# Moved denominator sums, moved stores and a new closing step in a two-layer graph network

## The chip, the cores and the metric

The kernel runs on one core of a Trainium2 chip. The metric is the device time of one execution in microseconds; lower is better. Before the change three executions took 3256.42, 3258.72 and 3258.72 us; the median is 3258.72. One further execution was recorded by the hardware profiler: it took 3257.38 us, of which the profile's span covers 3255.6.

The engines are named as in the profile: PE multiplies matrices (PEld loads its weights), DVE and ACT work element by element on 128 partitions, POOL and SP are used here mainly to issue DMA transfers. A name with a q (ACTq, SPq, POOLq) is an engine's instruction queue, where it issues a transfer.

## The reference

Two graph layers act on 4096 nodes with 512 features (4 heads of 128). The mask `adj` is the same 4096 x 4096 matrix of zeros and ones in both. Cut to what matters:

```python
h = relu(layernorm(x))
# layer 0: two attentions with the same weights, an MLP after each
Xw  = einsum('hnd,hde->hne', heads(h), W)
sig = sigmoid(f1[:, :, None] + f2[:, None, :])     # f1, f2 = Xw . V
att = softmax of sig where adj != 0, else 0        # both masks are adj
Xn  = batchnorm(att @ Xw)                          # the encoder attention
emb = batchnorm(elu(Xn @ Wenc.T + b) + Xn)
Yc  = elu((att @ emb) @ W.T)                       # the decoder attention
x   = x + batchnorm(elu(Yc @ Wdec.T + b) + Yc)
# layer 1: graph attention
h = relu(layernorm(x))
feats  = einsum('nf,hfo->hno', h, W1)
logits = leaky_relu(e_s[:, :, None] + e_n[:, None, :], 0.2)
attn   = softmax of logits where adj != 0
out    = x + relu(attn @ feats + b)
```

## The kernel before

All node data stand transposed: features on partitions, nodes along the row. A softmax is never formed as such. The kernel makes unnormalised weights, multiplies the values with them on PE, sums the weights over the source nodes (the denominator), and multiplies the products by the reciprocal of that sum.

**Stages.** Features (layer norm, transposes and the products with W, lines 465 to 552); encoder attention; the encoder's MLP and the decoder's values; decoder attention; the decoder's MLP, the residual and the second layer's features; graph attention (GAT). The three attentions share the function `attention` (L221). In the features' stage the products of two heads stand side by side in one PSUM bank, 130 columns each (128 values and 2 scores); L541 copies the values of each head to `R[0]` to `R[3]`, on ACT but for the last copies, which DVE makes. The order of instructions on an engine is the order of the program, except where the scheduler that builds the kernel finds another; `issue_after` and `pinned` keep an instruction behind a named one.

**Blocks and tiles.** An attention has 8 blocks, one for each head and half of the target nodes (2048). A block has 32 tiles, one for each 128 source nodes. A tile of weights `e` is 128 x 2048 floats. It is made by ACT and masked by DVE: in the encoder and decoder a tanh (L450) and an exp (L451) on ACT and a product with the mask (L452) on DVE; in the GAT a relu (L905) on ACT and one DVE instruction (L906) that adds, and masks. The mask tile `a` (bytes) is loaded by SP (L210) into one of five buffers. PE then multiplies: four matmuls of 512 columns for each tile (L371; for the first two tiles of a block the fourth follows at L368, since its PSUM bank is still in use by the block before). In the last block of the encoder and of the GAT the last tiles (one and two) are held back as `late` and multiplied bank by bank at L423.

**The program's order.** Weights of a tile are made in the order of the loop, with 8 buffers for `e` in the encoder, 6 in the decoder, 9 in the GAT, two of them shared by all three, so that the next attention's first two tiles can be made while the one before ends. What is done with a block's results is put into a list, `later`, and called some tiles into the next block.

**Denominators.** For each block the encoder and the GAT say which tiles are summed how:

```python
moved, by_ones, *ends_later = modes(n) if modes is not None else ((), ())
```

A tile in `moved` is added into a second accumulator (`acc2` in the encoder, `w` or a part of `R[2]` in the GAT) by two accumulating DMAs that POOL issues (L386). A tile in `by_ones` is summed by PE: four matmuls with ones (L262). All others DVE adds into `acc` (L392, L394). At the block's end PE sums the accumulators in the same way. The tables are ENC_FIRST for the encoder's first block, ENC_SECOND for its second (n = 1), ENC for the six after these; GAT_FIRST, GAT (six middle blocks) and GAT_LAST for the GAT. The decoder has no sums: it reads the reciprocals of the encoder. The reciprocals of a block take a way through DRAM in the next block, a "hop": copied, written, read back in another shape, inverted, written, and spread over the partitions (L269, L274, L278, L282, L287), by POOL's queue in the encoder and decoder, by ACT's in the GAT.

**Kept tiles.** Every fifth masked tile of the encoder (j = 4, 9, ...) is stored to DRAM, `ekeep`, three tiles after it was made, by ACT's queue (L358, and L410 and L412 for the last of a block), and loaded by SP in the decoder (L343) in place of being made again.

**A last block** has no next one. In the encoder and the GAT the denominators are copied on DVE with a lower bound (in the GAT with a small number added) and inverted (L434, L435), then PE spreads each bank's reciprocals over the partitions by a matmul with `ident` (L440). In the GAT each bank then takes four operations: ACT copies it out of PSUM with `ssum` added (L911), DVE multiplies (L915), ACT adds the bias with a relu (L918), DVE adds the residual (L921); then it is stored.

## Time and profile before

| what | us |
| --- | --- |
| median of the three runs | 3258.72 |
| profiled execution | 3257.38 |
| its span in the profile | 3255.6 |
| features, start to 66 | 66 |
| encoder attention, 62 to 1047 | 985 |
| encoder's MLP and decoder's values, 1047 to 1217 | 170 |
| decoder attention, 1217 to 2077 | 860 |
| decoder's MLP, residual, second features, 2077 to 2330 | 253 |
| GAT, 2330 to 3256 | 926 |

The stages overlap by a few tiles, and their bounds are rounded. Busy time in two of the stretches (start:end, length, then the busy time of PE, PEld, DVE, ACT and POOL with the number of instructions, the granted clock of PE, the busy share of the 16 DMA engines and the GB/s that they moved):

```
1028.00:1047.00 19.00, 16.70 (x62) 6.09 (x60) 16.15 (x12) 9.72 (x11) 0.00 (x0) 1.00 0.37 121
2330.00:3256.00 926.00, 915.97 (x2305) 394.94 (x2303) 897.16 (x451) 572.67 (x337) 197.78 (x232) 1.00 0.90 214
```

Three further forms of line are used below. A group is a set of instructions of one kind on one line (line, engine, operation, the output and input tiles, size, then busy time, count, mean time of one). In a list of waits stand the waiting instruction, an arrow, the instruction that released it, and the sum in us, the number and the longest of such waits. In a timeline stand the start, the length, the engine with the line, the tiles, the count of like instructions in a row, and in brackets how long the engine stood before and for whom.

### The profile page before, as it was taken

The numbers are of one execution on the slowest core, as the hardware profiler recorded it, in microseconds if no ns is written. First come the engines' busy times: TensorE is split into PE (matmuls) and PEld (weight loads), VectorE is DVE, ScalarE is ACT, GpSimd is POOL, SyncE is SP. The second block draws the span as 40 slices with busy tenths as digits, with TensorE's granted clock in tenths as the row PEclk, the third lists the DMA queues.
The fourth block names the chain that finished last, engine by engine and source line by source line (L and its number), as shares of the span: only waits on it lengthen the run. The fifth ranks groups of instructions, "written<-read, shape, count | busy, mean of one in ns | idle before, by whom it ended". The sixth has DMA issues, their size and how long they took to land.

```text
span 3255.6 us, 26153 instructions
## 1 busy us (share of the span) xinstructions
PE 3197.0 (98%) x8755; PEld 1483.5 (46%) x8755; DVE 2661.1 (82%) x1953; ACT 2597.9 (80%) x1884; POOL 478.7 (15%) x622
## 2 busy tenths in 40 slices
PE   7999999999999999999999999999999999999999
PEld 6334434444444464444444444448644444444443
DVE  7999999999999665556655665585699999999998
ACT  7999999999997459899999999566765666666664
POOL 2001211211211000000000000025412222222221
PEclk9999999999999999999999999999999999999999
DMA  9998988988986023433443443231489999889985
GB/s 210 197 196 229 268 227 224 270 230 220 271 234 162 2 68 132 146 129 133 145 147 120 137 155 121 77 123 58 128 204 219 219 226 241 220 206 236 221 216 142
DMA packets 211153, 578.51 MB, mean 178 GB/s; under 512 B 25069, under 2 KB 28173, under 8 KB 195017
## 3 DMA queue, kind: packets, MB, share of 16 engines
q0 software_dynamic: 67968, 222.51, 36.0%
q1 hardware_dynamic: 126432, 293.72, 26.5%
q10 hardware_dynamic: 16616, 60.60, 4.8%
q8 instruction: 69, 1.13, 0.1%
q14 instruction: 68, 0.55, 0.0%
HBM read 377.10 MB, written 84.29 MB: 142 GB/s over the span
## 4 chain that ended last, share of the span: by engine, by line
PE 67%; DVE 15%; issue 7%; ACT 6%; DMA 5%; POOL 0%; DVEq 0%; ACTq 0%; POOLq 0%
PE ps L371 51%; DVE e L452 9%; PE ps L615 7%; PE ps L811 3%; ACT e L450 3%; DMA a<-mask 3%; DVE acc L394 2%; ACT e L451 2%; DMA acc<-e 1%; PE den L262 1%; DVE R L394 1%; PE ps L672 1%; DVE e L906 1%; PE ps L368 1%; PE ps L537 1%
## 5 line engine op out<-in xcount | busy, mean ns | idle before, releaser
L371 PE MATMUL ps<-e,R 128*128 128x512 f32 x6024 | 2612.8, 594 | 34.8 <-DVE e L452 32.6
L371 PEld LDWEIGHTS ps<-e,R 128*128 128x128 f32 x6024 | 1139.8, 190 | 1500.7 <-issue 1398.1
L452 DVE TENSOR_TENSOR e<-e,a 128x2048 f32<-128x2048 f32 (+1 forms) x470 | 1052.2, 2261 | 391.2 <-ACT e L451 373.5
L450 ACT ACTIVATE e<-rowb,score 128x2048 f32<-128x2048 f32 (+1 forms) x470 | 912.3, 1967 | 86.2 <-PE ps L371 45.6
L451 ACT ACTIVATE e<-e 128x2048 f32<-128x2048 f32 (+1 forms) x470 | 870.5, 1879 | 6.1
L905 ACT ACTIVATE e<-rowb,nq,jcol 128x2048 f32<-128x2048 f32 x224 | 461.9, 2090 | 273.5 <-DMA w<-e 124.9
L906 DVE SCALAR_TENSOR_TENSOR e<-e,jcol,a 128x2048 f32<-128x2048 f32 (+1 forms) x265 | 593.6, 2280 | 7.7 <-ACT e L905 7.7
L394 DVE TENSOR_TENSOR acc<-acc,e 128x2048 f32<-128x2048 f32 x126 | 288.1, 2286 | 2.0
L394 DVE TENSOR_TENSOR R<-R,e 128x2048 f32<-128x2048 f32 x123 | 282.1, 2294 | 0.0
L386 POOL DMA_DIRECT2D w<-e x178 | 150.7, 849 | 612.5 <-DMA w<-e 356.3
L615 PE MATMUL ps<-R,w 128*128 128x512 f32 x512 | 220.3, 592 | 0.7 <-DVE w L573 0.7
L386 POOL DMA_DIRECT2D acc<-e x144 | 120.7, 883 | 536.5 <-DMA acc<-e 193.0
L287 POOL DMA_DIRECT2D rb<-rinvs x60 | 34.6, 582 | 1060.8 <-DVE R L563 867.5
L615 PEld LDWEIGHTS ps<-R,w 128*128 128x128 f32 x512 | 97.2, 190 | 122.7 <-issue 117.9
L636 ACT ACTIVATE ex<-ps,bias 128x512 f32<-128x512 f32 x64 | 44.0, 688 | 98.5 <-PE ps L615 78.7
L811 PE MATMUL ps<-w1x,hT 128*128 128x260 f32 x512 | 115.5, 384 | 1.4 <-ACT hT L789 1.4
L811 PEld LDWEIGHTS ps<-w1x,hT 128*128 128x128 f32 x512 | 96.5, 190 | 19.9 <-issue 3.3
L905 ACT ACTIVATE e<-w,nq,jcol 128x2048 f32<-128x2048 f32 (+1 forms) x41 | 67.4, 1710 | 24.9 <-DMA R<-e 24.9
L638 DVE SCALAR_TENSOR_TENSOR ex<-ex,re 128x512 f32<-128x512 f32 x64 | 45.0, 703 | 36.4 <-ACT re L637 36.2
L848 POOL TENSOR_TENSOR vacc<-vacc,R 128x128 f32<-128x128 f32 x120 | 65.9, 579 | 45.2 <-ACT R L841 44.8
L841 ACT ACTIVATE R<-ps,rstd 128x128 f32<-128x128 f32 x128 | 38.7, 371 | 29.2 <-PE ps L811 25.4
L262 PE MATMUL den<-e,ones 128*32 128x512 f32 x456 | 54.9, 598 | 0.0
(173 smaller groups left out, 1246.5 us busy)
## 6 DMA issues: line engine op xcount, KB each, us to landing
a<-mask SPq DMA_DIRECT2D x720, 256.0 KB, 4.2
w<-e POOLq DMA_DIRECT2D x178, 512.0 KB, 6.7
acc<-e POOLq DMA_DIRECT2D x144, 512.0 KB, 6.7
ekeep<-e ACTq DMA_DIRECT2D x48, 1024.0 KB, 7.8
e<-ekeep SPq DMA_DIRECT2D x48, 1024.0 KB, 4.8
mask<-in_adjT POOLq DMA_DIRECT2D x8, 2048.0 KB, 102.3
rowb<-rows SPq DMA_DIRECT2D x16, 1024.0 KB, 7.0
rb<-rinvs POOLq DMA_DIRECT2D x60, 256.0 KB, 4.0
```

Source lines behind the costliest of these rows:

```text
L262: last_ones = nc.tensor.matmul(den[s * 32:(s + 1) * 32, :], ones[:, 0:32], t[:, s * IB:(s + 1) * IB], start=start, stop=stop)
L371: last_main = nc.tensor.matmul(b, block(values[h], j), e[:, s * IB:(s + 1) * IB], start=(j == 0), stop=(j == NJ - 1))
L386: nc.gpsimd.dma_start(into_half, e_half, **({"accum_op": ALU.add} if j > moved[0] else {}))
L394: nc.vector.tensor_add(acc, acc, e)
L450: nc.scalar.activation(e, rowb, AF.Tanh, bias=column(score[:, 1], j, h), scale=0.5)
L451: last_act = nc.scalar.activation(e, e, AF.Exp, scale=0.5)
L452: last_dve = nc.vector.tensor_mul(e, e, a)
L615: last = nc.tensor.matmul(z, w[:, fb, o * P:(o + 1) * P], nodes(src[fb], ib), start=(fb == 0), stop=(fb == C - 1))
L811: m = nc.tensor.matmul(banks[k][:, 0:2 * DX], hT[:, fb, c * P:(c + 1) * P], w1x[:, fb, 2 * k:2 * k + 2, :].rearrange("p h x -> p (h x)"), ...
L848: nc.gpsimd.tensor_add(vacc[:, h, :], vacc[:, h, :], block(v1[h], j))
L905: last_act = nc.scalar.activation(e, rowb, AF.Relu, bias=column(nq, j, h), scale=column(jcol, j, h))
L906: last_dve = nc.vector.scalar_tensor_tensor(e, e, column(jcol2, j, h), a, ALU.add, ALU.mult)
```

## The change

- The copies out of PSUM: `R[0]` to `R[4]` become parts of one tile `RS`, and one instruction copies the values of two heads (104 copies on ACT become 52, 24 on DVE become 12).
- The encoder attention may start behind the features' last copy on ACT, `last_copy`, in place of the last relu; in the built order the tanh table's load and a quarter of the first tile's tanh then stand ahead of the last four relus.
- ENC_SECOND: other tiles in both lists, and seven moved tiles in place of six.
- From the third block on the stores of kept tiles go from ACT's queue to SP's, five tiles after their tile was made in place of three (36 of 48 stores), as do those left at a block's end.
- In the encoder's last block the additions of tiles j >= 26 that DVE makes (26 to 29) are put off to the last tile; in the built order the masks of 27 to 29 stand ahead of them, one addition follows, then the masks of 30 and 31, then three additions.
- The decoder's first two masks are kept behind a `bn_stats` in the encoder's MLP (`behind`).
- GAT: the middle blocks sum tile 31 alone by PE, tile 30 by DVE. The last block sums 30 and 31 by PE in place of 12, and holds back four tiles in place of two.
- The GAT's last block ends in `finish_gat`: the reciprocals go to DRAM and are spread back by SP's queue into `R[2]`, each bank takes two DVE instructions that read PSUM directly, and the bias is added to the residual beforehand. The matmuls at L440 and the ACT operations fall away there.

```diff
@@ -60,13 +60,13 @@
-ENC_SECOND = (13, 15, 17, 20, 22, 25), (5, 6, 10, 11, 23, 24, 30, 31)
+ENC_SECOND = (12, 14, 17, 19, 22, 24, 26), (1, 2, 4, 5, 7, 8, 30, 31)
 ENC = (0, 2, 5, 7, 10, 12, 15, 17, 20, 22, 25), (8, 9, 30, 31)
 GAT_FIRST = (0, 2, 4, 6, 8, 10, 12, 14, 16, 18, 20, 22, 24), (30, 31)
-GAT = tuple(range(3, 28, 2)), (30, 31), True
-GAT_LAST = (3, 5, 7, 9, 11, 13, 15, 17, 19, 21, 23), (12,)
+GAT = tuple(range(3, 28, 2)), (31,), True
+GAT_LAST = (3, 5, 7, 9, 11, 13, 15, 17, 19, 21, 23), (30, 31)
@@ -92,7 +92,8 @@
-    R = [big.tile([P, N], FP, name=f"R{i}") for i in range(5)]
+    RS = big.tile([P, 5, N], FP, name="R")
+    R = [RS[:, i, :] for i in range(5)]
@@ -326,7 +330,7 @@
-            adds, held, stores, next_row = [], [], [], None
+            adds, held, stores, at_end, next_row = [], [], [], [], None
             for j in range(NJ):
@@ -348,14 +352,16 @@
-                    with pinned(products_of[:1] if kept == "read" and n == 0 and j < 8 else []):
+                    with pinned([*(products_of[:1] if kept == "read" and n == 0 and j < 8 else ()),
+                                 *(behind if n == 0 and j < EP else ())]):
                         products_of = weights(e, rowb, a, j, h, SB if NJ * n + j < in_parts0 else 1)
+                    if stores and (store if n > 1 else j % KEEP == KEEP - 3):
+                        k, t = stores.pop()
+                        (nc.sync if n > 1 else nc.scalar).dma_start(ekeep[h][tb][k], t)
                     if store:
                         stores.append((j // KEEP, e))
-                    if j % KEEP == KEEP - 3 and stores:
-                        k, t = stores.pop()
-                        nc.scalar.dma_start(ekeep[h][tb][k], t)
                 def products():
@@ -373,7 +379,7 @@
-                if last and invert is not None and j >= NJ - (1 if kept is not None else 2):
+                if last and invert is not None and j >= NJ - (1 if kept is not None else 4):
@@ -388,10 +394,16 @@
-                        if len(adds) == 2:
+                        if last and kept is not None and j >= NJ - 6:
+                            at_end.append(e)
+                        elif len(adds) == 2:
                             nc.vector.tensor_add(acc, *adds)
...
                             nc.vector.tensor_add(acc, acc, e)
+                    if j == NJ - 1:
+                        for t in at_end:
+                            nc.vector.tensor_add(acc, acc, t)
                     if held and j + 1 not in by_ones:
@@ -407,9 +419,9 @@
                 if last:
-                    nc.scalar.dma_start(ekeep[h][tb][k], t)
+                    nc.sync.dma_start(ekeep[h][tb][k], t)
                 else:
-                    at(EVICT, nc.scalar.dma_start, ekeep[h][tb][k], t)
+                    at(EVICT, (nc.sync if n > 1 else nc.scalar).dma_start, ekeep[h][tb][k], t)
             if not last:
@@ -422,7 +434,7 @@
-            outs = [out(spool, h, tb, s, po[s]) for s in range(SB)]
+            outs = [out(spool, h, tb, s, po[s]) for s in range(SB)] if finish_last is None else po
             if invert is None:
@@ -435,6 +447,15 @@
+            elif finish_last is not None:
+                nc.sync.dma_start(rinvs[h][tb].rearrange("o (s i) -> (o s) i", i=IB), inv[0:P:32, :])
+                rbs = [rb for rb, in in_parts(SB, acc)]
+                for s, rb in enumerate(rbs):
+                    nc.sync.dma_start(rb, everywhere(rinvs[h][tb], 0, s * IB, IB))
+                for s, rb in enumerate(rbs):
+                    finish_last(h, tb, s, po[s], rb)
+                continue
             for s, o in enumerate(outs):
@@ -537,8 +558,11 @@
-                            by_dve = ib + h >= NIB - 1
-                            (nc.vector.tensor_copy if by_dve else nc.scalar.copy)(block(R[2 * k + h], j), pv[:, h, 0:D])
+                        by_dve = ib + k >= NIB - 1
+                        copied = (nc.vector.tensor_copy if by_dve else nc.scalar.copy)(
+                            RS[:, 2 * k:2 * k + 2, j * D:(j + 1) * D], pv[:, :, 0:D])
+                        if not by_dve:
+                            last_copy = copied
@@ -596,7 +620,7 @@
         with tc.tile_pool(name="enc", bufs=1) as spool:
-            with tc.issue_after(last_act.ins), tc.issue_after(masks0[-1][1].ins):
+            with tc.issue_after(last_copy.ins), tc.issue_after(masks0[-1][1].ins):
                 attention("enc", keep, spool, tanh_weights, R[0:4], lambda h, tb: (rows[tb], h), out_enc,
@@ -641,8 +665,8 @@
-                    nc.vector.bn_stats(stats[:, o, ib, :], d)
-                    between(o, ib)
+                    made = nc.vector.bn_stats(stats[:, o, ib, :], d)
+                    between(o, ib, made)
@@ -654,7 +678,10 @@
-            mlp_block(work, w, xc, yc, "enc_mlp_bn_gamma", "enc_mlp_bn_beta", a_att, lambda o, ib: None, last_head)
+            behind_it = []
+            mlp_block(work, w, xc, yc, "enc_mlp_bn_gamma", "enc_mlp_bn_beta", a_att,
+                      lambda o, ib, made: behind_it.append(made) if (o, ib) == (1, 0) else None, last_head)
             for h in range(H):
@@ -702,7 +729,7 @@
             attention("dec", keep, spool, tanh_weights, xc, lambda h, tb: (rows[tb], h), out_dec, (scaled, elu), 4,
-                      kept="read", extras={(1, 6): sums_of_weights, (1, 16): bias_of_decoder})
+                      kept="read", behind=behind_it, extras={(1, 6): sums_of_weights, (1, 16): bias_of_decoder})
@@ -916,12 +943,15 @@
-        dst = nodes(outT[h * P:(h + 1) * P, :], tb * SB + s)
-        if last:
-            nc.vector.tensor_add(o, o, x1_last[0][:, s * IB:(s + 1) * IB])
-            nc.sync.dma_start(dst, o)
-        else:
-            nc.gpsimd.dma_start(dst, o, accum_op=ALU.add)
+        nc.gpsimd.dma_start(nodes(outT[h * P:(h + 1) * P, :], tb * SB + s), o, accum_op=ALU.add)
+    def finish_gat(h, tb, s, po, rb):
+        x1b, nb = x1_last
+        o = R[2][:, TB + s * IB:TB + (s + 1) * IB]
+        nc.vector.scalar_tensor_tensor(o, po, ssum[:, h:h + 1], rb, ALU.add, ALU.mult)
+        nc.vector.scalar_tensor_tensor(o, o, nb, x1b[:, s * IB:(s + 1) * IB], ALU.max, ALU.add)
+        nc.sync.dma_start(nodes(outT[h * P:(h + 1) * P, :], tb * SB + s), o)
     with tc.tile_pool(name="gat", bufs=1) as spool:
@@ -929,12 +959,18 @@
+            x1_last.append(edge.tile([P, 1], FP, name="nb"))
+            nc.vector.tensor_scalar_mul(x1_last[1], vec_of("b")[:, H - 1:H], -1.0)
+        def add_bias(load):
+            nc.scalar.activation(x1_last[0], x1_last[0], AF.Identity, bias=vec_of("b")[:, H - 1:H])
         with tc.issue_after(last_pe.ins):
...
                       (N * TINY, ALU.add), sums=R[2][:, 0:TB], sums2=(row0, R[2][:, TB:N]), row0=row0, in_parts0=3,
-                      extras={(0, 1): rest_of_rows, (H * NTB - 1, NJ - 10): load_last})
+                      extras={(0, 1): rest_of_rows, (H * NTB - 1, NJ - 10): load_last, (H * NTB - 1, NJ - 4): add_bias},
+                      finish_last=finish_gat)
```

More of the change, by code (lines that the diff above doesn't have):

```diff
@@ L221, in attention @@
     def attention(what, keep, pools, weights, values, row_of, out, finish, ebufs, modes=None, invert=None,
-                  kept=None, sums=None, sums2=None, extras={}, row0=None, masks0=(), in_parts0=1):
+                  kept=None, sums=None, sums2=None, extras={}, row0=None, masks0=(), in_parts0=1,
+                  finish_last=None, behind=()):
         spool, made, masks0 = pools, 0, list(masks0)
@@ L519 @@
                         last_pe = nc.tensor.transpose(pt[:, fb, :], hn[:, fb * P:(fb + 1) * P], ident)
-                    last_act = nc.scalar.activation(hT[:, :, c * P:(c + 1) * P], pt, AF.Relu)
+                    nc.scalar.activation(hT[:, :, c * P:(c + 1) * P], pt, AF.Relu)
                 if ib == 0:
@@ L735, in residual, with between @@
             return added
-        def between(o, ib):
+        def between(o, ib, made):
             if o in (1, 2):
```

## Prediction

> **What bounds the kernel now.** I read the page's first part, then stretches by stage, then the waits and the timeline of the engine that each stage hangs on.
>
> ```profile
> PE 3197.0 (98%) x8755; PEld 1483.5 (46%) x8755; DVE 2661.1 (82%) x1953; ACT 2597.9 (80%) x1884; POOL 478.7 (15%) x622
> ```
>
> PE's 98% is an average, so it doesn't say which stage a change can shorten. The stretches do (start:end, length, then the busy time of PE, PEld, DVE, ACT, POOL; granted clock; DMA share):
>
> ```profile
> 9.00:66.00 57.00, 52.77 (x387) 47.70 (x387) 46.19 (x184) 44.27 (x148) 23.49 (x16) 1.00 1.06 213
> 62.00:1028.00 966.00, 935.01 (x2499) 398.90 (x2498) 920.70 (x531) 955.12 (x524) 148.00 (x193) 1.00 0.91 231
> 1047.00:1203.00 156.00, 155.28 (x563) 85.59 (x564) 108.15 (x188) 63.81 (x84) 2.25 (x4) 1.00 0.07 22
> 1217.00:2077.00 860.00, 859.67 (x2023) 382.56 (x2024) 503.82 (x288) 787.53 (x458) 15.24 (x29) 1.00 0.39 133
> 2455.00:2569.00 114.00, 114.00 (x290) 49.32 (x289) 114.00 (x56) 70.21 (x41) 25.69 (x31) 1.00 0.94 222
> 2797.00:2911.00 114.00, 114.00 (x290) 49.34 (x289) 110.41 (x55) 72.09 (x42) 25.64 (x31) 1.00 0.94 221
> ```
>
> Features (9 to 66 us): PE, with 4.2 us of gaps. Encoder attention (62 to 1028): ACT, 955.1 of 966; it makes a tile in 3.69 us (tanh 1.89, exp 1.80, start to start), 118.1 a block of 32. MLP and decoder attention: PE. Graph attention: PE and DVE both. In its second block DVE is full, in its fifth it still needs 110.4 of 114.
>
> ACT's waits in the encoder are few:
>
> ```profile
> ACT e L450 <- DVE e L452: 6.3, 2, 4.6
> ACT e L450 <- DVE R L563: 4.0, 1, 4.0
> ACT e L450 <- PE den L262: 0.8, 1, 0.8
> ```
>
> The longest one, on ACT's timeline:
>
> ```profile
> 218.41 0.35 ACTq L358 DMA_DIRECT2D ekeep<-e  x1
> 218.81 3.90 ACT L450 ACTIVATE e<-rowb,score 128x2048 f32<-128x2048 f32 x2 [4.61 <-DVE e L452]
> ```
>
> The store of the second block's tile 4 stands in ACT's queue and waits for DVE to mask that tile; the tanh behind it stands too. DVE is late there because of additions to the denominators.
>
> **Features: one copy for two heads, weights begun earlier.** 104 ACT copies of 128x128 (23.4 us busy, 0.225 each) become 52 of 128x256. That size has no row; between 0.225 and the 0.516 of a 128x512 copy (L681, 16.5 us for 32) a line gives 0.322, in all 16.7: ACT is freed of 6.7 us. But PE sets this stage, and only gaps that end on a copy (0.7 on DVE, 0.4 on ACT) can go: 0.8 us taken. In the new order ACT loads the tanh table (1.28) and makes a quarter of tile 0 (0.66) before the last four relus. It is the same ACT work; what goes is 0.4 us of ACT idle around those relus. Together 1.2 us. Bounds: -1.5, when the last features, now behind 1.9 us on ACT, also hold up DVE's first masks; and 2.7, if most of PE's gaps go.
>
> **Encoder blocks 1 and 2.** In block 2 the tiles summed by TensorE move to 1, 2, 4, 5, 7, 8. Until tile 8 DVE then has 2 additions instead of 6, 4 x 2.2 = 8.8 us less; 2 of the 3 in front of tile 4's mask go, 4.4 us, so the mask ends at 214.0 instead of 218.4, and ACT gets there at 214.2. The second wait (4.0, at 274.8) ends within 0.1 us of a landing of the addition of tile 15, which POOL issued only at 260.2, behind the hop of the reciprocals. Now tiles 12 and 14 are issued ahead of that hop, and 17, the next, is wanted two tiles later. Of 8.6 us I take 7. Bounds 3 (the second wait comes back on tile 17) and 9.6 (all ACT idle). The seventh DMA addition goes to POOL, which has 612 us of idle before such issues; it takes one addition (2.2 us) off DVE.
>
> **36 stores from ACT's queue to SP's.** An issue is 0.33 us of ACT's sequencer, but activations run on without a gap (a store at 143.32 lies inside an exp from 142.79 to 144.59). Saved: 0. The price lies on SP, where mask loads now stand behind stores:
>
> ```profile
> a<-mask SPq DMA_DIRECT2D x720, 256.0 KB, 4.2
> ekeep<-e ACTq DMA_DIRECT2D x48, 1024.0 KB, 7.8
> ```
>
> By these rows a mask lands in 4.2 us and nothing is in front of it. The Trainium skill (DMA: Bandwidth & Descriptors, Queues, rings and completion order) speaks against the move: an engine consumes one ring's descriptors in order, while it alternates between rings, so a load behind a store on SP waits for it, which one behind ACT's did not. With the rule a load takes up to 7.8 + 4.2 = 12.0 us. It is issued five tiles ahead, 5 x 3.69 = 18.4 us. So the sum has 0 by row and by rule; the cover is 6.4 us.
>
> **Encoder's end.** The last block's additions of tiles 26 to 29 go behind masks:
>
> ```profile
> 1028.73 4.61 DVE L394 TENSOR_TENSOR acc<-acc,e 128x2048 f32<-128x2048 f32 x2
> 1033.26 6.89 DVE L452 TENSOR_TENSOR e<-e,a 128x2048 f32<-128x2048 f32 x6
> 1042.94 0.69 DVE L434 TENSOR_SCALAR dsb<-den 128x512 f32<-128x512 f32 x1 [2.79 <-PE den L262]
> ```
>
> ACT had tile 31 ready at 1027.7, DVE masked it until 1037.7. With the masks first: 27 to 29 end at 1024.1, one addition fits while tile 30 comes (1025.9), 30 and 31 end at 1030.8, three additions at 1037.4. PE then runs from tile 26 at 1019.6 without its waits: five tiles x 3.43 = 1036.7, four sums x 0.9 = 1040.3. The denominator stands 2.6 us earlier (bounds 0 and 4.4, to DVE's 1037.4). What PE does next follows. The decoder's first two masks, which stood in between (part of the x6, and one at 1054), are pinned into the MLP, where DVE has 48 of 156 us free; without that cover they cost 4.7 us.
>
> **Graph attention.** Six middle blocks sum one tile less on TensorE: 24 matmuls, x24 in 2.71 us for three tiles in the chain, so 0.9 per block, 5.4 in all. DVE gets an addition in each, 2.2 us. The starts of the last masks of the first three blocks, 2438.87, 2549.06, 2659.26, show DVE's own period, 110.2. After: DVE 112.4, PE 113.97 - 0.9 = 113.1. In steady state PE still sets the pace, but DVE gains 0.7 us a block on PE, where it gained 3.8. In the last block (18 additions, 2 over a middle block before) this decides: DVE begins its last mask at 2438.9 + 6 x 112.4 + 114.6 = 3227.9 and ends it at 3230.2. PE wants tile 30 for its sums at 3131.1 - 5.4 + 28 x 3.43 + 1.2 = 3223.0. So PE stands some 5 us, and the end hangs on DVE.
>
> From 3230.2: three sums (tile 31, the moved ones, DVE's), 2.7, to 3232.9; before, 3238.6.
>
> ```profile
> 3238.54 7.13 PE L423 MATMUL ps<-e,R 128*128 128x512 f32 x16
> 3245.51 3.60 PE L440 MATMUL ps<-dsb,ident 128*128 128x512 f32 x8
> ```
>
> Then PE has 15 matmuls of the last four tiles left, x 0.86 = 12.9, to 3245.8, and no L440. Beside it: DVE's copy and reciprocal, 4.1, to 3237.0; the reciprocals to DRAM 1.8 (row of rinvs<-dsb), 3238.8; spread back, 4.0 (row rb<-rinvs on POOL's queue, the same transfer): 3242.8 to 3243.9. DVE's eight closing operations (0.6 apart, against twelve on DVE and ACT before) end at 3248.0, the last pair waiting for nothing but DVE. From the last addition to the end it took 3255.6 - 3252.44 = 3.2. So 3251.2: 4.4 us gained. Here the skill's price differs from the row (same page, Anatomy of one DMA: 2.0 us fixed plus bytes over 436 GB/s, an estimate of 2.6 us for 256 KB): rb at 3241.4, DVE done right after PE at 3247.3, the end at 3250.5, 5.1 us. I take the row. The dearest row (ACT's queue, 6.9) gives 3253.9, 1.7 us.
>
> **Sum.** 1.2 + 7 + 0 + 2.6 + 4.4 = 15.2 us. The profiled execution took 3257.4 (its span and 1.8 around it): 3242.2. The median of the runs is 1.3 above it, so 3243.5.
>
> **Rivals.**
> 1. The front gives nothing: masks, which land 12 to 19 us after issue while the mask casts run, hold DVE, and ACT's waits return with the earlier start. Then 1.2 + 7 is lost, 2.6 + 4.4 stay: 3251.7. For it: DVE waited 6.7 us for masks there. Against it: ACT's waits trace to the store and the additions.
> 2. DVE isn't the bound of graph attention, so PE doesn't stand in its last block: 5 us more, 3238.5. For it: DVE idled 3.6 us a block late in the stage. Against it: the period of 110.2.
> 3. Slower: masks behind stores on SP. Beyond 18.4 us a load stalls DVE once per store, 36 times; the gain is used up at 15.2 / 36 = 0.42 over, 18.9 us. At 20 us: 3243.5 + 36 x 1.6 = 3301. For it: loads took 12 to 19 us where the DMA share was 1.05; against it: the cover of 6.4 us, and 4.2 in the median.
> 4. Changes nothing that can be told: the front lost, the encoder's end lost too (0), graph attention at its dearest row, 1.7: 3257.
>
> **How the numbers follow.** Forecast 53%, rival 1 25%, rival 2 10%, rival 3 4%, rival 4 8%. This kernel can be told from no change beyond 0.2%, 6.5 us. Forecast and rivals 1 and 2 are faster (3251.7 by 7 us): 0.88; rival 4 is within; rival 3 slower. The lower end adds the better ends of front (2.6) and end (0.7) to rival 2: 3236 rounded; the upper end covers rival 1: 3253. Rivals 3 and 4 lie outside.
>
> **What would show it.** ACT's tanh of block 2 without a wait at its first store; the encoder's last reciprocal some 11 us earlier; DVE near 112.4 us a block through all six middle blocks; PE waiting some 5 us for masks shortly before the last sums; rb landing before PE's last matmul ends. Wrong if mask loads wait for stores, if ACT's waits in blocks 1 to 3 still sum to 8 us, or if DVE has idle time left in the middle blocks.

## The result and the profile after

The changed kernel takes 3244.53 us (median of 6 runs, 3242.20 to 3245.74), the kernel before 3257.93 in the same comparison (6 runs): 13.4 us less, a ratio of 0.9959 with a 95% interval of 0.9948 to 0.9970. The forecast was 3243.5. The profiled spans are 3255.6 and 3243.0, so 12.6 us are there to be found in the traces.

The line of the page of the changed kernel that gives busy time and instructions of each engine, and the stretches of features and encoder attention (columns as before: PE, PEld, DVE, ACT, POOL, clock, DMA share, GB/s):

```profile
PE 3189.8 (98%) x8707; PEld 1480.1 (46%) x8707; DVE 2665.7 (82%) x1946; ACT 2582.4 (80%) x1825; POOL 478.3 (15%) x624
...
9.00:66.00 57.00, 50.89 (x393) 47.60 (x394) 46.63 (x176) 43.16 (x100) 23.70 (x16) 1.00 1.06 215
62.00:1028.00 966.00, 942.70 (x2499) 400.17 (x2498) 920.91 (x519) 955.30 (x528) 150.00 (x195) 0.99 0.92 234
```

ACT is as full in the encoder as before (955.3 of 966, before 955.1), although the two stalls that the prediction removed are gone. ACT's waits in the encoder (62 to 1040) say why: others have come.

```profile
ACT e L471 <- PE den L266: 4.5, 4, 2.0
ACT e L471 <- DMA acc<-e: 2.7, 2, 2.5
ACT e L472 <- DVE e L473: 2.7, 3, 1.3
ACT e L471 <- issue: 0.6, 1, 0.6
```

They sum to 10.5 us; before, 11.1. Where the gain lies is read by setting the same event of both timelines beside each other (us):

| event | before | after | gain so far | forecast so far |
| --- | --- | --- | --- | --- |
| exp of tile 3, first block, ends | 79.7 | 76.0 | 3.7 | 1.2 |
| exp of tile 31, second block, ends | 312.2 | 302.9 | 9.3 | 8.2 |
| exp of tile 31, third block, ends | 430.9 | 428.1 | 2.8 | 8.2 |
| the encoder's last exp ends | 1027.7 | 1022.0 | 5.7 | 8.2 |
| the encoder's last reciprocal begins | 1043.7 | 1034.6 | 9.1 | 10.8 |
| the GAT's first mask begins | 2328.8 | 2319.7 | 9.1 | 10.8 |
| end of the span | 3255.6 | 3243.0 | 12.6 | 15.2 |

The sum of the forecast is near. Its terms are not: 6.5 us are lost in the third block, and 2.9 come back in blocks four to eight, where nothing was forecast. The experiments are about these two, the features, and the two ends.

### The profile page after: what moved, and what is told of

The parts are those of the page before. It is cut to its first block, busy times and chain, and to the rows that moved or that the text cites. A ratio compares the mean times of both kernels' runs of the same rounds, so it can differ in the third digit from the quotient of the medians.

```text
span 3243.0 us, 26057 instructions
## 1 busy us (share of the span) xinstructions
PE 3189.8 (98%) x8707; PEld 1480.1 (46%) x8707; DVE 2665.7 (82%) x1946; ACT 2582.4 (80%) x1825; POOL 478.3 (15%) x624
## 4 chain that ended last, share of the span: by engine, by line
PE 50%; DVE 26%; issue 13%; DMA 6%; ACT 4%; DVEq 0%; POOL 0%; ACTq 0%; POOLq 0%; SPq 0%
PE ps L377 36%; DVE e L933 8%; DVE R L402 8%; PE ps L639 7%; DVE e L473 4%; DVE acc L402 3%; PE ps L838 3%; DMA a<-mask 3%; DMA acc<-e 2%; ACT e L471 2%; ACT e L472 1%; DMA w<-e 1%; PE den L266 1%; PE ps L699 1%; PE ps L374 1%
## 5 line engine op out<-in xcount | busy, mean ns | idle before, releaser
L402 DVE TENSOR_TENSOR R<-R,e 128x2048 f32<-128x2048 f32 x128 | 292.3, 2283 | 0.0
L402 DVE TENSOR_TENSOR acc<-acc,e 128x2048 f32<-128x2048 f32 x121 | 276.3, 2283 | 0.9
```

The lines of the kernel that those rows point to most:

```text
L402: nc.vector.tensor_add(acc, acc, e)
```

## The experiments

Medians, with the change against the changed kernel's 3244.53, and the profiled span:

| kernel | median | change | span |
| --- | --- | --- | --- |
| the second block's old lists | 3245.99 | +1.5 | 3244.3 |
| second block without six sums on PE | 3244.60 | +0.1 | 3241.6 |
| six mask buffers | 3241.84 | -2.7 | 3237.6 |
| stores back on ACT's queue | 3254.14 | +9.6 | 3250.2 |
| two copies, behind both matmuls | 3244.79 | +0.3 | 3244.5 |
| two copies, each behind its matmuls | 3246.92 | +2.4 | 3244.9 |
| begun behind the last relu | 3244.18 | -0.4 | 3242.0 |
| encoder's last additions not put off | 3247.42 | +2.9 | 3245.7 |
| GAT's tile 30 on PE again | 3244.64 | +0.1 | 3243.3 |
| GAT's last block, tile 25 by DMA | 3243.63 | -0.9 | 3241.5 |
| old closing step | 3249.08 | +4.6 | 3247.2 |
| six mask buffers and the eased last block | 3240.54 | -4.0 | 3240.0 |

Single executions of a kernel differ by 2.2 to 7.5 us here, and the kernel before, run beside each group of these, took 3257.5 to 3258.2. So differences below some 2 us are read from the traces, event by event, and not from the medians.

### The second block, and who sets the third

```diff
-ENC_SECOND = (12, 14, 17, 19, 22, 24, 26), (1, 2, 4, 5, 7, 8, 30, 31)
+ENC_SECOND = (13, 15, 17, 20, 22, 25), (5, 6, 10, 11, 23, 24, 30, 31)
```

> The changed kernel with the encoder's second block summed by the old lists (ENC_SECOND as before), all else as changed. Theory A, the prediction's: ACT sets the encoder, and the new lists save it 7 us; then this kernel takes 3244.5 + 7 = 3251.5 us, and the encoder's last denominator stands 7 us later (1040.9 in place of 1033.9). Theory B: PE sets the encoder's first two blocks (it has no gap from 190 to 301 us in the changed kernel), ACT's stalls there were covered by PE, and all that reached the end of the third block is the 3.7 us of the features; then it takes 3243.6 to 3245.0 us, the last denominator stays within 1 us of 1033.9, and ACT has its two stalls in the second block back (8 us) but loses the 6.5 us of waits in the third.

The old lists bring both stalls back, as the prediction read them (ACT's timeline, the bracket is the stand before the instruction):

```profile
216.68 3.90 ACT L471 ACTIVATE e<-rowb,score 128x2048 f32<-128x2048 f32 x2 [3.66 <-DVE e L473]
273.11 2.00 ACT L471 ACTIVATE e<-rowb,score 128x2048 f32<-128x2048 f32 x1 [4.33 <-DMA acc<-e]
```

Yet ACT ends the third block only 1.8 us later (429.9), and 0.7 of that was there in the features already. Theory A is out: 7 us became about 1. Theory B, that PE sets these blocks, came nearer (its last denominator, due within 1 us of 1033.9, stands at 1035.7). It was tested by taking six of PE's sums away; the block's denominators then lack these tiles.

```diff
-                        held.append(e)
+                        held.extend([] if kept == "write" and n == 1 and j < 9 else [e])
```

> The changed kernel without the sums of tiles 1, 2, 4, 5, 7 and 8 in the encoder's second block: PE has 5.4 us less there, nothing takes their place, and that block's denominators lack these tiles. Theory B: PE sets the encoder's first two blocks, the sums of the DMA accumulator start 5.4 us earlier (at 317.3 in place of 322.7), the chain of DMA additions in the third block with them, and ACT's 7.2 us of waits in that block shrink to under 2: ACT ends tile 31 of the third block at some 422.7 in place of 428.1, and the time is 3244.5 - 5.4 = 3239.1. Theory A, the prediction's: ACT sets the encoder and PE's sums are off its path; no difference.

Theory B is out too: PE is busy 4.7 us less between 180 and 460 (269.0 us, in the changed kernel 273.7), yet ACT ends the third block at 428.9. PE only stands more (11.0 us of gaps there, in the changed kernel 6.3), for DVE's masks. A third theory took the loads of the masks, for which DVE waits 12.0 us in the changed kernel (6.7 before).

```diff
-        return keep.tile([P, TB], U8, name="a", bufs=5)
+        return keep.tile([P, TB], U8, name="a", bufs=6)
```

> The changed kernel with six mask buffers in place of five (and, for the room, two buffers in place of three for the encoder's spread reciprocals); the order on PE, DVE and ACT is the same. Theory C: the encoder's first two blocks are set by mask loads, which land late beside the mask casts; in the changed kernel DVE waits 12.0 us for them, in ten places, the longest 2.9 us. A load that is issued one tile (3.7 us) earlier covers all of these: DVE's waits for masks fall below 3 us, ACT ends tile 31 of the third block 5 to 7 us before 428.1, and the time is 3237.5 to 3239.5. Theory D: the DMA engines are full there (busy share 1.05), so loads issued earlier land no earlier; DVE's waits for masks stay near 12 us and the time within 1 us of 3244.5.

It lies between the theories: ACT ends the third block 3.3 us sooner (424.8), the time falls by 2.7 us. But the masks are not how. DVE's waits in the first two blocks, in this kernel:

```profile
DVE e L473 <- DMA a<-mask: 7.0, 8, 3.0
DVE dcol L282 <- DMA dcol<-dens: 6.6, 1, 6.6
```

DVE waits 5 us less for masks and 6.6 for a column of denominators instead; the second block's last mask ends at 316.0, not sooner than in the changed kernel (314.6). The 3.3 us stand in POOL's queue, at the start of the third block. First the changed kernel, then the one with six mask buffers:

```profile
328.74 0.88 POOL L392 DMA_DIRECT2D acc<-e  x1 [0.89 <-DMA acc<-e]
329.28 0.90 POOL L273 DMA_DIRECT2D dens<-dsb  x1
341.28 0.57 POOL L278 DMA_DIRECT2D dcol<-dens  x1 [11.10 <-DMA dens<-dsb]
341.84 1.82 POOL L392 DMA_DIRECT2D acc<-e  x2
```

```profile
330.47 0.90 POOL L273 DMA_DIRECT2D dens<-dsb  x1
337.92 0.59 POOL L278 DMA_DIRECT2D dcol<-dens  x1 [6.55 <-DMA dens<-dsb]
338.50 1.82 POOL L392 DMA_DIRECT2D acc<-e  x2
```

The hop of the reciprocals writes the denominators to DRAM and waits for them to land before it reads them back; the accumulating DMAs of the moved tiles stand behind that wait on POOL. In the third block these DMAs are a chain, each waiting for the one before (13 waits, 40.0 us, from 320 to 425), and their tiles hold the buffers that ACT wants. The time from the issue of the chain's second pair to ACT's exp of tile 31:

| kernel | second pair | exp of tile 31 ends | apart |
| --- | --- | --- | --- |
| before | 345.8 | 430.9 | 85.1 |
| second block's old lists | 343.1 | 429.9 | 86.8 |
| stores on ACT | 343.1 | 429.3 | 86.2 |
| without six sums | 342.3 | 428.9 | 86.6 |
| changed | 341.8 | 428.1 | 86.3 |
| six mask buffers and eased last block | 339.0 | 426.6 | 87.6 |
| six mask buffers | 338.5 | 424.8 | 86.3 |

In these seven, whatever was edited, ACT ends the block some 86 us behind that pair; in the other seven kernels with a profile it is 86.1 to 87.5. Before the change ACT came late enough not to wait for the chain: it has no stand in the block, and its 85.1 is its own pace. Now it came 9.3 us early, the chain 4.0 early, and ACT stood for the rest, among other places here:

```profile
320.78 2.01 ACT L471 ACTIVATE e<-rowb,score 128x2048 f32<-128x2048 f32 x1 [1.22 <-PE den L266]
359.79 2.01 ACT L471 ACTIVATE e<-rowb,score 128x2048 f32<-128x2048 f32 x1 [1.97 <-PE den L266]
400.35 2.01 ACT L471 ACTIVATE e<-rowb,score 128x2048 f32<-128x2048 f32 x1 [2.46 <-DMA acc<-e]
```

The first two of these ended with PE's sums by the profile, the third with a landing of the chain. Behind that third one ACT has no stand left in the block. In every profile but that of the kernel before, the last stand of ACT in this block ended so, at 399.8 to 402.6 us in ten of them, at 380 to 399 in the other three. The chain of work that the profile follows back agrees: in the changed kernel it goes from the second pair over one accumulating DMA after another (7.7 to 9.6 us each), and once over a second wait of the hop (9.2 us from 350.9, for the inverted denominators to land), into ACT's tanh at 400.35.

So the chain sets ACT there. No kernel moved the hop alone, so how much of it is the hop's is open. Nor is it shown what shortened POOL's wait from 11.1 to 6.55 us: POOL's order up to there is the same, the wait is 8.4 to 11.9 us in the other kernels with five mask buffers and 6.2 in the other with six, and from 325 to 345 us SP's queue moved 3.67 MB in the changed kernel and 2.57 in this one. That the small write waits for SP's transfers is a guess from this. Kernels that are alike up to the third block end it between 428.0 and 430.3, so a us or two of these differences is chance; their second pairs, at 341.8 to 344.2, shift with it.

### The stores

```diff
-                    if stores and (store if n > 1 else j % KEEP == KEEP - 3):
-                        k, t = stores.pop()
-                        (nc.sync if n > 1 else nc.scalar).dma_start(ekeep[h][tb][k], t)
                     if store:
                         stores.append((j // KEEP, e))
+                    if j % KEEP == KEEP - 3 and stores:
+                        k, t = stores.pop()
+                        nc.scalar.dma_start(ekeep[h][tb][k], t)
```

> The changed kernel with all stores of kept tiles back on ACT's queue, three tiles after their tile. Theory A, the prediction's: a store on ACT's queue costs ACT nothing, so 3244.5 us, no difference. Theory B: each of the some 30 stores in blocks 3 to 8 holds ACT 0.1 us (ACT's lead over the kernel before grows by 0.57 us in each block of six stores), so 2.9 to 3.4 us more: 3247.4 to 3247.9, with ACT's lead over the kernel before constant from the fourth block on. A third: mask loads behind stores on SP cost time in the changed kernel; then this one is faster than 3244.5.

The costliest part to undo, by far: 9.6 us in the median, 7.2 in the span (the profiled execution is the second fastest of twelve). By the traces, ACT's last exp ends 4.0 us later (1026.0; 1.2 of it stand at the end of the third block already), and the reciprocal behind it 3.4 more (1042.0). Theory B's 2.9 to 3.4 us is near the first number, but its reason is not the one. The timeline of ACT, stores on ACT:

```profile
484.71 3.88 ACT L471 ACTIVATE e<-rowb,score 128x2048 f32<-128x2048 f32 x2
488.50 1.89 ACT L472 ACTIVATE e<-e 128x2048 f32<-128x2048 f32 x1
489.05 0.33 ACTq L364 DMA_DIRECT2D ekeep<-e  x1
490.30 1.89 ACT L472 ACTIVATE e<-e 128x2048 f32<-128x2048 f32 x1
492.10 1.99 ACT L471 ACTIVATE e<-rowb,score 128x2048 f32<-128x2048 f32 x1
494.12 1.91 ACT L472 ACTIVATE e<-e 128x2048 f32<-128x2048 f32 x1
495.93 3.88 ACT L471 ACTIVATE e<-rowb,score 128x2048 f32<-128x2048 f32 x2
```

and of the changed kernel:

```profile
483.50 3.70 ACT L472 ACTIVATE e<-e 128x2048 f32<-128x2048 f32 x2
487.10 3.89 ACT L471 ACTIVATE e<-rowb,score 128x2048 f32<-128x2048 f32 x2
490.89 3.70 ACT L472 ACTIVATE e<-e 128x2048 f32<-128x2048 f32 x2
494.49 3.89 ACT L471 ACTIVATE e<-rowb,score 128x2048 f32<-128x2048 f32 x2
```

The store is free: from 488.50 to 490.30 it is 1.80, as from exp to exp without one. What costs is the order. In the changed kernel ACT works two tiles at a time: two tanhs, two exps. With the stores on its queue a lone tanh with its own exp right behind it comes between the pairs, and that exp begins 2.02 us after its tanh (492.10 to 494.12), not 1.89, and the next tanh 1.82 after it, not 1.80. From 440 to 1000 us this kernel has 19 spacings of 2.02 or 2.03 from tanh to exp (the kernel before 19 of 2.01 or 2.02, the changed one none), and 18 of 1.82: 19 x 0.13 + 18 x 0.02 = 2.8 us. The distance of the two timelines grows by 2.6 us (from 1.15 at 443 to 3.75 at 985). So the order that the scheduler made around the stores cost ACT its 0.6 us a block, and moving them mended it.

The other 3.4 us lie at the encoder's end.

### The encoder's end

```diff
-                        if last and kept is not None and j >= NJ - 6:
+                        if False:
```

> The changed kernel with the last additions of the encoder not put off (on DVE an addition follows each of four masks, the mask of tile 31 comes last); the order elsewhere is the same. If the new order is worth what the prediction says (2.6 us), or what it measured against ACT's end (3.4 us: 11.9 in place of 15.2 us from ACT's last exp to the denominator), the sums on PE then come behind the last mask: it ends at 1032.2, two sums of tiles and one of the accumulator take 3.6, so the denominator stands at 1035.8 in place of 1033.9 and the time is 3246.5. If ACT's earlier end did it, not the order: 3244.5.

From ACT's last exp to the reciprocal it took 16.0 us before, 12.6 in the changed kernel, 13.7 here, and 16.0 with the stores on ACT. The order of DVE in the changed kernel, and with the stores on ACT:

```profile
1009.83 8.88 DVE L473 TENSOR_TENSOR e<-e,a 128x2048 f32<-128x2048 f32 x4
1018.63 2.28 DVE L406 TENSOR_TENSOR acc<-acc,e 128x2048 f32<-128x2048 f32 x1
1020.83 4.48 DVE L473 TENSOR_TENSOR e<-e,a 128x2048 f32<-128x2048 f32 x2
1025.23 6.93 DVE L406 TENSOR_TENSOR acc<-acc,e 128x2048 f32<-128x2048 f32 x3
1033.86 0.69 DVE L446 TENSOR_SCALAR dsb<-den 128x512 f32<-128x512 f32 x1 [1.70 <-PE den L266]
```

```profile
1027.07 4.61 DVE L406 TENSOR_TENSOR acc<-acc,e 128x2048 f32<-128x2048 f32 x2
1031.59 4.49 DVE L473 TENSOR_TENSOR e<-e,a 128x2048 f32<-128x2048 f32 x2
1041.27 0.69 DVE L446 TENSOR_SCALAR dsb<-den 128x512 f32<-128x512 f32 x1 [5.19 <-PE den L266]
```

In the last three of these kernels DVE ends its last item 10 us behind ACT's last exp (in the kernel before 12.5, with masks of the decoder in between); what differs is which item is last. If the masks of tiles 30 and 31 are, PE still has a tile to multiply and DVE stands 5.19 us; if only tile 31's is, 2.99; if additions are, 1.70. The kernel with the stores on ACT puts the additions off in the program too, but the scheduler placed them ahead of the masks. So 1.1 us (13.7 to 12.6) belong to the additions put off in the order that the changed kernel has, and the remaining 2.3 to how the masks and additions of these tiles came to be placed. Expected were 2.0 us more, measured 2.8 in the span, of which 2.2 had come before the last exp already. The pinning of the decoder's first masks was not taken out alone.

### The features

```diff
-                        copied = (nc.vector.tensor_copy if by_dve else nc.scalar.copy)(
-                            RS[:, 2 * k:2 * k + 2, j * D:(j + 1) * D], pv[:, :, 0:D])
+                        for h in range(2):
+                            by_dve = ib + h >= NIB - 1
+                            copied = (nc.vector.tensor_copy if by_dve else nc.scalar.copy)(
+                                block(R[2 * k + h], j), pv[:, h, 0:D])
```

> The changed kernel with one copy for each head out of PSUM (104 on ACT and 24 on DVE), all else as changed. Theory A, the prediction's: the merged copies are worth 0.8 us, since PE sets the features' stage: the last transposes start 0.8 us later than 56.97. Theory B: in the values' half of each 512 nodes ACT's copies set the pace (16 x 0.245 us against 8 x 0.435), and the merged copies are worth 2.5 us: the last block of transposes starts at 59.5 and the encoder's first tanh 2.5 us later than 58.4. The time by A 3245.3, by B 3247.0 if the encoder passes the front on.

The start of the stage varies (the second 512 nodes' transposes begin between 17.5 and 21.1 us in kernels that are alike up to there), so the stretch from the second to the eighth begin of transposes is read: 39.87 us before, 36.98 in the changed kernel, 37.43 here. Merging two copies is worth 0.45 us; neither theory's number, and not where the 2.9 us are. The next kernel has the copies where they were, each directly behind its own head's matmuls:

```diff
                             nc.tensor.matmul(pv[:, h, :], hT[:, 2 * k + h, c * P:(c + 1) * P], w0x[:, 2 * k + h, :],
                                              start=True, stop=True)
+                            by_dve = ib + h >= NIB - 1
+                            copied = (nc.vector.tensor_copy if by_dve else nc.scalar.copy)(
+                                block(R[2 * k + h], j), pv[:, h, 0:D])
```

> The changed kernel with the copies of the features as before: one for each head, each directly behind its head's matmuls in the program, but R in one tile as changed. The kernel with two copies behind both matmuls kept the gain of the features. Theory E: the gain is that the second head's matmul no longer waits for the copy of the first from the same bank; PE waits for ACT's copies 2.8 us again, the last block of transposes starts at 59.4 in place of 57.0, and the encoder's tile 11 ends 2.4 us later than 105.6, at 108.0. Theory F: one tile for R does it; then 57.0 and 105.6 stay. In the time at most 1 us of either is seen, since blocks 1 to 3 pass little of the front on.

39.86 us: all is back, and so are PE's waits, absent both in the changed kernel and with two copies behind both matmuls. PEld's list in this kernel, between 8 and 60 us:

```profile
PEld ps L558 <- ACT R L562: 2.5, 11, 0.5
```

Theory E holds: with copy and matmul in turn on one bank, the second head's matmul waits for the first head's copy (of the 33 weight loads of this line that a copy on ACT released in the kernel before, 21 are the second head's). The merged copy can only stand behind both matmuls; that, and not the shorter work on ACT, is most of its gain. The median lies 2.4 us behind the changed kernel's, more than the 1 us that was expected to be seen.

```diff
-            with tc.issue_after(last_copy.ins), tc.issue_after(masks0[-1][1].ins):
+            with tc.issue_after(last_act.ins), tc.issue_after(masks0[-1][1].ins):
```

(`last_act` is the last relu again.)

> The changed kernel with the encoder's weights begun behind the features' last relu as before. Theory A, the prediction's: the earlier start is worth 0.4 us: 3244.9. Theory B: the part of the front that the copies do not explain, 3.7 - 2.5 = 1.2 us, is the earlier start: 3245.7, with the exp of tile 3 at 77.2 in place of 76.0.

The exp of tile 3 ends at 78.4 although the last transposes began 0.55 us sooner: the earlier start is worth 2.9 us at that tile and 1.1 at tile 11. By tile 11 of the second block nothing is left of it (225.9 in both).

### The graph attention

```diff
-GAT = tuple(range(3, 28, 2)), (31,), True
+GAT = tuple(range(3, 28, 2)), (30, 31), True
```

> The changed kernel with tile 30 of the six middle blocks of the graph attention summed by PE again. Theory A, the prediction's: PE needs 0.9 us a block more (it gained 0.86 us in each of the six in the changed kernel, 5.2 in all), but DVE is 2.2 us a block less busy, keeps its lead, and PE's stand of some 5 us for masks ahead of the last sums goes; the two cancel: 3244.5 + 5.2 - 5.1 = 3244.6, PE without a gap in the last block. Rival: DVE does not set the end of the last block, and the 5.2 us come back in full: 3249.7.

The two cancel, as the prediction's reading says: 3244.64. Of PE's stands one short one is left (1.13 us), where theory A had none. The six sums were worth 0.4 us at most (923.7 us from the GAT's first mask to the end, in the changed kernel 923.3), since the last block hangs on DVE. PE in the changed kernel:

```profile
3216.81 1.94 PE L266 MATMUL den<-e,ones 128*32 128x512 f32 x8 [2.34 <-DVE e L933]
3218.68 1.78 PE L435 MATMUL ps<-e,R 128*128 128x512 f32 x2
3221.28 1.06 PE L266 MATMUL den<-e,ones 128*32 128x512 f32 x8 [0.82 <-DVE e L933]
```

The first sum and the two matmuls behind it take 3.7 us here, because PE's clock was at half from 3216.6 to 3220.0 us (shown in the last section); in the kernel with six mask buffers the same work takes 2.1, at full clock, and PE's second stand is 2.34 us in place of 0.82. Both kernels then reach DVE's copy of the denominators 904.5 us after the GAT's first mask. So the slow clock cost nothing here: it filled time in which PE would have stood for DVE's last mask.

```diff
-                      extras={(0, 1): rest_of_rows, (H * NTB - 1, NJ - 10): load_last, (H * NTB - 1, NJ - 4): add_bias},
-                      finish_last=finish_gat)
+                      extras={(0, 1): rest_of_rows, (H * NTB - 1, NJ - 10): load_last})
```

(and `add_to_output` as before)

> The changed kernel with the old closing step of the last block (reciprocals spread by matmuls with the identity, four operations for each bank on ACT and DVE), all else as changed. Theory A, the prediction's: the matmuls come behind the late ones, PE ends 3.6 us later (3240.7), and the last operations 3.3 after that, 3244.0 in place of 3239.6: 4.4 us slower, 3248.9. Rival: the way through DRAM, for which DVE stands 5.05 us in the changed kernel, costs what the matmuls did: within 1 us of 3244.5.

3249.08, as theory A says. With the old closing DVE stands for the matmuls with the identity, with the new one for the reciprocals from DRAM, half as long:

```profile
3238.60 0.69 DVE L942 TENSOR_TENSOR R<-R,ps 128x512 f32<-128x512 f32 x1 [10.28 <-PE ps L461]
```

```profile
3233.34 0.75 DVE L952 SCALAR_TENSOR_TENSOR R<-ps,ssum,R 128x512 f32<-128x512 f32 x1 [5.05 <-DMA R<-rinvs]
```

From the GAT's first mask to the end it is 926.8 us before, 923.3 changed, 928.6 with the old closing: by that the closing step gains 5.4 us, and the rest of the GAT's edits give 1.8 of them back. But 1.2 us of both are chance: with the old closing the clock fell to half at 3221.5, during the last sums, and DVE's copy of the denominators comes 905.7 us after the first mask, not 904.5. Without that the closing step gains 4.2, near theory A's 4.4, and the rest gives 0.6 back.

```diff
-GAT_LAST = (3, 5, 7, 9, 11, 13, 15, 17, 19, 21, 23), (30, 31)
+GAT_LAST = tuple(range(3, 26, 2)), (30, 31)
```

> The changed kernel with one tile more (25) in the last block of the graph attention added by DMA, so one addition less on DVE (2.2 us). If DVE's masks set the end of that block, the last mask ends 2.2 us earlier, and the end comes 1.6 us earlier (PE sums tiles 30 and 31 back to back here, so it loses 0.6 to a longer stand): 3242.9. If PE sets it, no difference; if the DMA chain, which then lands at some 3213 of the sums' 3222, sets it, slower.

0.6 us by the same measure (922.7), less than the 1.6 expected: DVE is ready sooner, but PE now stands 3.40 us in one piece, and runs at a lower clock behind it:

```profile
3218.20 1.18 PE L266 MATMUL den<-e,ones 128*32 128x512 f32 x8 [3.40 <-DVE e L933]
3219.14 1.96 PE L266 MATMUL den<-w,ones 128*32 128x512 f32 x8
3220.85 1.84 PE L266 MATMUL den<-R,ones 128*32 128x512 f32 x8
```

PE begins to sum tile 31 899.4 us after the GAT's first mask, 2.2 sooner than in the changed kernel (901.6), but the three sums take 4.4 us in place of 2.7. The last kernel adds to this, and to the six mask buffers, that three tiles are held back, so that PE has tile 28 to multiply meanwhile.

```diff
-                if last and invert is not None and j >= NJ - (1 if kept is not None else 4):
+                if last and invert is not None and j >= NJ - (1 if kept is not None else 3):
```

> The kernel with six mask buffers, and with the last block of the graph attention eased: tile 25 too is added by DMA, and three tiles in place of four are held back, so that PE multiplies tile 28 where it stood for DVE. If PE's stand there costs its 3.2 us and the clock that falls behind it (0.62 granted from 3217 to 3221 us, some 1.5 us), PE doesn't stand over 1.2 us, the granted clock stays at 1.00, and the end comes 2.5 us sooner than in the kernel with six mask buffers alone: 3242.0 if the mask buffers bring nothing, 3235 to 3237 if they bring what theory C says. If the closing operations, which then wait for the reciprocals alone, take it all: less than 1 us.

```profile
3218.01 1.06 PE L266 MATMUL den<-e,ones 128*32 128x512 f32 x8
3219.24 1.07 PE L266 MATMUL den<-e,ones 128*32 128x512 f32 x8 [0.16 <-DVE e L933]
```

PE stands 0.16 us, and the GAT takes 920.1 us, 2.7 less than with six mask buffers alone (922.9), as expected. The gain is not the stand that went, but DVE: the sum of tile 31 begins 2.2 us sooner, as with tile 25 alone, and no slow clock follows. Of the 2.7 us the medians show 1.3 (single executions lie between 3237.6 and 3242.9). It is the fastest kernel of the study: 3240.54, 0.9949 of the kernel before (0.9936 to 0.9961); the 3235 to 3237 that the third theory would have given were not reached.

## Why the prediction was right in its number and wrong in its parts

- **Features, 1.2.** Measured 2.9 in the stage and 3.7 at the first tiles, above its upper bound of 2.7. The failed step is "only gaps that end on a copy (0.7 on DVE, 0.4 on ACT) can go". Each of these matmuls is drawn 0.28 us long while the next can begin 0.11 after it, so a wait of up to 0.17 leaves no gap in PE's busy time; the waits were in the list of PE's weight loads (2.4 us on PEld, 11 times), which was not read. The earlier start, put at 0.4, was worth 1.1 at tile 11. The merged copy takes 0.37 us, not 0.32.
- **Encoder blocks 1 and 2, 7.** The step held where it was looked at: both stalls go, ACT gains 5.6 us more by the end of the second block. The failed one is the silent next: that this lead lasts. Its sentence on the second wait, an addition "which POOL issued only at 260.2, behind the hop of the reciprocals", named the very queue, and it was not asked what the same hop does one block later. The chain there had moved 4.0 us, and ACT got 2.8 in all. Rival 1 said that the front gives nothing; its waits came (12.0 us of DVE for masks), and most of its loss, but by the chain of accumulating DMAs and not by the masks. (POOL's 612 us of idle in the prediction are those of the GAT's row; the encoder's row has 536.5, which changes nothing.)
- **Stores, 0.** Right for the issue on ACT and for the loads on SP, wrong in the sum: 2.9 us in blocks four to eight, through the order of tanh and exp. The mask loads land as fast as ever, and in blocks four to eight DVE has no wait for one (issues, KB, us to landing):

```profile
a<-mask SPq DMA_DIRECT2D x720, 256.0 KB, 4.1
...
ekeep<-e SPq DMA_DIRECT2D x36, 1024.0 KB, 7.0
```

  So rival 3 and the ring order that spoke against the move cost nothing: the cover of five tiles was enough. Loads do land later behind a store: of those whose landing the changed kernel's trace has from 440 to 1020 us, the eight issued within 2 us behind a store on SP took 4.6 to 9.9 us (median 7.6), the other 47 took 4.8 in the median. Whether they wait in the ring or share the engines with the store isn't separated.
- **Encoder's end, 2.6.** Measured 3.4, from the order forecast; but it came with the order that the scheduler found, not with the edit alone.
- **GAT, 4.4.** Measured 3.5. DVE's full blocks (112.4 us each; PE multiplies the last tile of a block 5.9, 6.7, 7.4, ... us behind the begin of its mask, so DVE's lead grows by 0.7 us a block), the stand, the sums at 3233.1 in the old frame (3224.06 + 9.07) for 3232.9 forecast and the last reciprocal's way are as worked out. The stand was 3.2 us of waiting and 1.5 of a slow clock, and 4.7 of waiting in the kernel with six mask buffers, for "some 5". The spread of the reciprocals let DVE go on 3.2 us after its issue, between the two prices, 4.0 and 2.6, that the prediction set side by side. Of the 0.9 us that are missing, 0.2 stand at the sums and most of the rest in PE's last matmuls and the closing operations, which end at 3248.7 in the old frame for 3248.0.
- Rival 2 is out (the stand is there), rival 4 too.

8.2 forecast against 2.8, then 0 against 2.9, 2.6 against 3.4 and 4.4 against 3.5: the number came near because misses cancelled in part, 12.6 for 15.2, and because the kernel before has a median of 3257.93 in six runs, 0.8 below the 3258.72 from which the forecast started. That part is luck. (The lower end of the range adds up to 3235.2, not 3236.)

## What to carry to other kernels

A stall removed is a lead, and a lead is kept only if every other queue that the next stage waits for has moved as far: follow the same queue one stage on. A transfer that costs its queue nothing can still change the order that a scheduler makes of the instructions around it; compare the orders, and price pairs and lone instructions from their spacing. And matmuls and copies on one bank are best written matmuls first: in turn, they held PE for ACT although their columns don't meet.

## What the runs showed of the hardware

A short stand of PE can be followed by a slow clock. Clock by stretch (the number ahead of the DMA share) behind the changed kernel's stand of 2.34 us, and in the kernel with six mask buffers behind a like stand of 2.33:

```profile
3216.00:3217.00 1.00, 0.19 (x4) 0.19 (x8) 1.00 (x2) 0.00 (x0) 0.00 (x0) 0.81 0.00 0
3217.00:3218.00 1.00, 1.00 (x8) 0.01 (x2) 1.00 (x1) 0.00 (x0) 0.00 (x0) 0.50 0.00 0
...
3220.00:3221.00 1.00, 0.46 (x1) 0.00 (x0) 1.00 (x1) 0.00 (x0) 0.00 (x0) 0.98 0.00 0
```

```profile
3212.00:3214.00 2.00, 1.92 (x10) 0.30 (x2) 2.00 (x2) 0.00 (x0) 0.00 (x0) 1.00 0.00 0
```

Half speed for some 3.4 us in one, none in the other. The Trainium skill (TensorE: Matmul & The Clock Gate, Part 1) states half rate after an idle window of about 3.4 us that runs freely, and so varies from run to run; the half rate and the variation agree, the stand of 2.34 us was shorter than that.

What it costs depends on the work behind it. In the changed kernel nothing: PE had to wait for DVE's last mask anyway. With tile 25 by DMA it came behind the last stand (3.40 us), on the sums that DVE waited for, and cost 1.7 us; with the old closing 1.2.

A like dip follows 3.6 us of one-column matmuls in the decoder in ten of the fourteen profiles (clock 0.72 from 1320 to 1324 in the changed kernel, 1.00 with tile 25 by DMA). The stretch from the first MLP's matmuls to the second's is 1025.3 us without it, 1027.0 with it (the kernel before and the changed one), and 1028.7 in the two profiles where it lasts twice as long: 1.7 us of chance in each span, and 3.4 between the spans of the two kernels with six mask buffers.
